# A two-layer graph kernel: the second layer's self weights folded at the start, seven early blocks, and the neighbour weights loaded behind the last store

## The chip, the cores and the metric

The kernel runs on one core of one Trainium2 chip. A core has five engines that run side by side, each in the order of its own queue: TensorE (PE: matmuls, and transposes written as matmuls), VectorE (DVE), ScalarE (ACT), GpSimd (POOL) and SyncE (SP, which here only issues transfers). Transfers (DMAs) are issued from the queues of SP, ACT and POOL. Engines and transfers wait for each other by semaphores. The metric is the device time of one execution in microseconds (us). The kernel before takes 694.12 us, the median of three runs (692.1 to 694.69).

## The reference

There are 4096 nodes with 512 features each, and an adjacency matrix of 4096 x 4096 int32 (64 MB) in which a node has about four neighbours. Layer 0 is a graph attention layer of 8 heads x 64, layer 1 averages neighbours; each is followed by a residual and a layer norm.

```python
# layer 0
Wh = einsum('nf,hfo->hno', x, W);  f1 = Wh . a[:, :64];  f2 = Wh . a[:, 64:]
e = where(adj > 0, leaky_relu(f1[:, :, None] + f2[:, None, :], 0.2), -9e15)
x = layernorm(x + heads_side_by_side(softmax(e) @ Wh))
# layer 1
agg = (adj > 0) @ x / max(degree, 1)
self_f = x @ W_self + b_self;  nb_f = agg @ W_nb + b_nb
x = layernorm(x + relu(concat(self_f, nb_f) @ W_comb + b_comb))
```

There is no nonlinearity between W_self, W_nb and W_comb. So with W_c1 and W_c2 the upper and the lower half of W_comb, layer 1 is relu(x (W_self W_c1) + agg (W_nb W_c2) + b), with b = b_comb + b_self W_c1 + b_nb W_c2. The kernel makes these two 512 x 512 products on the chip, once per execution.

## The kernel before

All work is cut into 32 blocks of 128 nodes. The queues of the engines are in the order in which the function `listed_layers` writes the operations down; nothing is reordered behind its back. Buffers come from pools that hand out the tiles of one name in turn, so an operation that writes a tile waits for the last reader of the tile that had its place. A second function with dense matmuls runs only when the lists of neighbours don't fit; it doesn't run on these inputs.

**Stage A, 0 to some 230 us: node rows and neighbour lists.** First come the heads' weights w_sb (1 MB, L817) and the first blocks of x and adj. `times` and `summed` (L838, L845) multiply W by a, so that one matmul gives a node's row: 512 features and its attention terms. The loop at L891 then runs over b = 0 to 29. In each iteration SP issues one block of x (256 KB, L314, eight blocks ahead) and adjacency block b+2 as two halves of 1 MB (`load_adj`, L384, four buffers named `at`). ACT turns each half into bf16 (`mask_adj`, L390), PE folds 128 x 4096 flags into 128 x 512 keys (`fold_adj`, L408) in a bank of PSUM that ACT fills first (`key_bank`, L400), DVE takes the largest keys (`max_keys`, L423) and decodes them to lists of neighbours (`decode`). Beside it PE transposes a block of x (`transposed`, L324) and multiplies it with W (`node_half`, L332, four matmuls of 128 x 264, twice per block), and ACT stores the row in table t0 (`store`, L885). POOL adds the blocks of x up for the row of nodes without neighbours (`sum_x`, L318). AHEAD holds the iterations that do one block of rows more. After the loop SP issues W_nb and W_c2 (`load_fold`, 2 MB, L250 and L252), the last row and the last two adjacency blocks follow, and m2 = W_nb W_c2 is made by `fold_weights`: four transposes per 128 rows (L269), a copy by ACT (L271), four matmuls of 128 x 512 (L281), a copy (L286). It is a generator: each `next` issues one piece.

**Stage B, to some 517 us: layer 0.** The loop at L967 runs over i = -2 to 32, with several blocks in different steps. POOL gathers the rows of neighbours from t0, five indirect DMAs per block (`gather`, L586), into GA = 5 buffers. A slot of 128 rows can be shared by the further neighbours of many nodes; PE adds those by a matmul with a matrix of owners (`a_shared`, L677). DVE and ACT do the softmax, weights, sums and layer norm. PE transposes the new x, SP stores it (xt, L722), and PE makes z = x m2 (`a_z`, L714), which SP stores in table t1 (L719). At i = 12 SP issues W_self and W_c1 (2 MB), and at i = 30 and 31 the bias is folded: `bias_column` (L292), `fold_bias` (four DVE operations, L300), `sum_bias` (PE, L308). While the last blocks are in work, POOL gathers for the first blocks of layer 1 (`gather_early`): from the part of t1 that is stored already (LE + b blocks for block b), with indices clamped to that limit (`lim`, `idxe`). What an early gather had to leave out is fetched by one further gather per early block (`gather_late`, NE of them).

**The seam and stage C, to the end: layer 1.** After the loop POOL issues the gathers of block 5 early and six late ones. PE makes m1 = W_self W_c1 by `fold_weights`, with `g_shared` of blocks 0 and 1 (L753) and `g_late` (L763) between its pieces, then `g_self` (x m1, L746) of blocks 0 and 1. The loop at L1082 runs over the 32 blocks: `g_self(b+2)`, `g_bias(b+3)`, `g_norm(b-1)`, `g_shared(b)`, `g_late(b)` for early blocks, `g_adds(b)`, the gathers of block b + GB into the buffer of block b (GB = 6 buffers), and `g_moments(b)` (L769, L773); `g_norm` also stores the block of the output.

Of the kernel before, what the change touches and what calls it, by code (L numbers as in the profile page):

```python
# [31 lines left out]
F32 = mybir.dt.float32  # L32
# [8 lines left out]
P = 128  # L41
# [9 lines left out]
KH = 2  # L51
# [3 lines left out]
GA = 5  # L55
GB = 6
NE = 6
LE = 26
G = 4
FMAX = 30.0  # L60
# [29 lines left out]
def listed_layers(  # L90
# [32 lines left out]
    EX = KX + 2 + 1  # L123
    AHEAD = (6, 12)
    FIRST = (0, 1, 3)
# [47 lines left out]
    for k in range(2):  # L173
# [53 lines left out]
        allow_small_or_imprecise_dtypes=True,  # L227
    )
    idxe = const.tile([P, NE, KS], U32, name="idxe")
    idxl = const.tile([P, NE], U32, name="idxl")  # L230
    esl = const.tile([P, NE, 2], F32, name="esl")
    endl = const.tile([P, NE], F32, name="endl")
    m2 = const.tile([P, FB, HD], F32, name="m2")
    brow = const.tile([P, HD], F32, name="brow")
# [12 lines left out]

    def load_fold(k, w, fp):
        wr = fp.tile([P, FB, HD], F32, name="wr")
        nc.sync.dma_start(wr, w.rearrange("(c p) o -> p c o", p=P))  # L250
        wc = fp.tile([P, FB, HD], F32, name="wc")
        nc.sync.dma_start(  # L252
            wc, w_comb[k * HD : (k + 1) * HD, :].rearrange("(c p) o -> p c o", p=P)
        )
        return wr, wc

    def load_bias(k):
        brw = small.tile([FB, P], F32, name="brw", bufs=1)
        nc.scalar.dma_start(brw, (b_self, b_nb)[k].rearrange("(c p) -> c p", p=P))
        return brw  # L260

    def fold_weights(loaded, m, wp, tags):

        wr, wc = loaded

        def turned(c):
            tp = ps.tile([P, FB, P], F32, name="sm", bufs=2)
            for d in range(FB):
                nc.tensor.transpose(tp[:, d, :], wr[:, c, ts(d, P)], ident)  # L269
            wT = wp.tile([P, FW], F32, name="row", bufs=2)[:, 0:FIN]  # L270
            nc.scalar.copy(wT, tp.rearrange("p c r -> p (c r)"))  # L271
            return wT.rearrange("p (c r) -> p c r", c=FB)

        wT = turned(0)
        for c in range(FB):
            nxt = turned(c + 1) if c + 1 < FB else None
            yield
            tag = tags[c % 2]
            mp = ps.tile([P, HD], F32, name=tag, bufs=2 if tag == "pw" else 1)
            for d in range(FB):  # L280
                nc.tensor.matmul(  # L281
                    mp, lhsT=wT[:, d, :], rhs=wc[:, d, :], start=(d == 0), stop=(d == FB - 1)
                )
                if d % 2:
                    yield
            nc.scalar.copy(m[:, c, :], mp)  # L286
            wT = nxt

    def bias_column(k, brw):

        bt = ps.tile([P, FB], F32, name="sm", bufs=2)
        nc.tensor.transpose(bt, brw, ident[0:FB, 0:FB])  # L292
        bcol = small.tile([P, FB], F32, name=f"bcol{k}", bufs=1)
        nc.scalar.copy(bcol, bt)
        return bcol
# [303 lines left out]
    def gather_early(b, pool):  # L599
        return gather(t1[0 : 2 + (LE + b) * P, :], b, pool, idxe)  # L600

# [108 lines left out]

    def a_z(b, xT, wp):
        pz = ps.tile([P, HD], F32, name="pw", bufs=2)
        for c in range(FB):
            nc.tensor.matmul(  # L714
                pz, lhsT=xT[:, c, :], rhs=m2[:, c, :], start=(c == 0), stop=(c == FB - 1)
            )
        z = wp.tile([P, HD + 2 * H], F32, name="row", bufs=2)
        nc.scalar.copy(z[:, 0:HD], pz)
        nc.sync.dma_start(t1[2 + b * P : 2 + (b + 1) * P, :], z[:, 0:HD])  # L719
# [70 lines left out]
    wp = ctx.enter_context(tc.tile_pool(name="work", bufs=1))  # L790
    fp = ctx.enter_context(tc.tile_pool(name="fold", bufs=1, side="right"))
    oo_cm = tc.tile_pool(name="owners", bufs=1, side="right")
# [17 lines left out]

    av = fp.tile([P, FB, HD], F32, name="wr")
    nc.scalar.dma_start(
# [3 lines left out]
    for h in range(H):  # L816
        nc.sync.dma_start(  # L817
            w_sb[:, :, H + h * D : H + (h + 1) * D], w0[h].rearrange("(c p) o -> p c o", p=P)
        )
    load_x(0, nc.scalar)  # L820
    load_adj(0, ap)
    load_x(1)
    load_x(2)
    load_adj(1, ap)
    for b in range(3, XL):
        load_x(b)
    xacc = xa.tile([P, FIN], F32, name="xacc")
    nc.gpsimd.memset(xacc, 0.0)
# [5 lines left out]
    xT = transposed(0, wp)  # L834
    prs = fp.tile([P, FB, HD], F32, name="wc")

# [21 lines left out]
    summed(0, 1, pr1[0])  # L858
    summed(1, 1, pr1[1])
    for b in range(XL):  # L860
        sum_x(b, xacc)
# [15 lines left out]
    def on_last(b):  # L877
        if b % G == 0:
            last[0] = fp.tile([P, G, KH * P], F32, name="wr")
        return last[0][:, b % G, :]  # L880
# [3 lines left out]
    def store(w, row):  # L884
        nc.scalar.dma_start(t0[2 + w * P : 2 + (w + 1) * P, :], row[:, 0:TW])  # L885

    for h in range(NH):
        mask_adj(0, h)
    key_bank(0)
    w, row, lists = 0, None, []  # L890
    for b in range(LB):  # L891
        for k in range(1 + (b in AHEAD)):
            load_x(w + k + XL)
            sum_x(w + k + XL, xacc)
        load_adj(b + 2, ap)
        if b == 3:
            brw = load_bias(1)
            nc.vector.memset(brow, 0.0)
            nc.scalar.dma_start(brow[0:1, :], b_comb.rearrange("(a o) -> a o", a=1))
            pads(wp)  # L900
        some(lists)
        nxt = transposed(w + 1, wp) if w + 1 < NB else None
        if w > 0:
            store(w - 1, row)
        if b + 1 < LB:
            key_bank(b + 1)
            for h in range(NH):
                mask_adj(b + 1, h)
            row = node_block(w, xT, b)
            w, xT = w + 1, nxt  # L910
        if b in AHEAD:
            nxt = transposed(w + 1, wp)
            store(w - 1, row)
            row = node_block(w, xT)
            w, xT = w + 1, nxt
        if b == 5:
            bcol = bias_column(1, brw)
        if b == 24:
            pieces = mean_row(w_sb, xacc, wp)
        if b >= 24:  # L920
            next(pieces, None)
        if b == 14:
            lates = late_lists(dp, fp.tile([P, FB * HD // P, P], F32, name="wr"))
        if b >= 14:
            next(lates, None)
        if b % G == G - 1:
            lists = [*lists[-1:], decode(b + 1 - G, dp, on_own)]
    loaded = load_fold(1, w_nb, fp)
    row = node_block(w, xT)
    store(w, row)  # L930
    fold_adj(LB - 1, dp)
    max_keys(LB - 1)
# [4 lines left out]
    G0[0] = gather(t0, 0, gps[0])  # L937
    m2s = fold_weights(loaded, m2, wp, ("pw", "pw"))
    some(lists)
    for b in (LB, LB + 1):  # L940
        key_bank(b)
        for h in range(NH):
            mask_adj(b, h)
        some(lists)
        fold_adj(b, dp)
        max_keys(b)
# [18 lines left out]
    XT, G1 = {}, {}  # L965
    biased = fold_bias(loaded, bcol)
    for i in range(-2, NB + 1):  # L967
# [27 lines left out]
        if on(i - 1):  # L995
            a_z(i - 1, XT.pop(i - 1), wp)
        if i == -2:
# [13 lines left out]
        for k in range({-2: 1, -1: 3, 0: 2}.get(i, 0)):  # L1011
            next(m2s, None)
        if 1 <= i < 12:
            some(lists)
        if 1 <= i < 5:
            next(biased)
        if i == 12:
            loaded = load_fold(0, w_self, fp)
            brw = load_bias(0)
        if i == NB - 2:  # L1020
            bcol = bias_column(0, brw)
        if i == NB - 1:
            for _ in fold_bias(loaded, bcol):
                pass
            sum_bias()
    m1 = loaded[0]


    dp_cm.__exit__(None, None, None)
    oo_cm.__exit__(None, None, None)  # L1030
    gps = [gps[(NB + b) % GA] for b in range(GA)]
    gps.append(ctx.enter_context(tc.tile_pool(name="gat5", bufs=1)))
    gl = ctx.enter_context(tc.tile_pool(name="late", bufs=1)).tile([P, NE, HD], F32, name="gl")
    G1[GA] = gather_early(GA, gps[GA])
    for b in range(NE):
        gather_late(b, gl)
    for b in range(2):
        OWN[b] = owners(b, wp)
    m1s = fold_weights(loaded, m1, wp, ("key", "tp"))
    next(m1s)  # L1040
    for b in range(2):
        g_bias(b)
        g_first(b, G1[b])
        for k in range(2):
            next(m1s)
        g_shared(b, G1[b])
        g_adds(b, G1[b], wq)
        G1[b + GB] = gather(t1, b + GB, gps[b])
        next(m1s)
    xT = load_xT(0, wp)  # L1050
    for k in range(2):
        next(m1s)
    for b in range(2):
        g_late(b, gl, wq)
    for _ in m1s:
        pass
    for b in range(2):
        nxt = load_xT(b + 1, wp)
        g_self(b, xT, m1)
        xT = nxt  # L1060
    g_bias(2)
    for b in range(2):
# [439 lines left out]
```

## Time and profile before

The profiled execution took 771.3 us, 77 us longer than the median of the timed runs. Its span on the core is 769.6 us at a mean granted TensorE clock of 0.932.

| | us | share of the span |
|---|---|---|
| median of three runs | 694.12 | |
| profiled execution, span | 771.3, 769.6 | |
| PE busy | 643.8 | 84% |
| DVE busy | 497.8 | 65% |
| ACT busy | 438.8 | 57% |
| POOL busy | 381.1 | 50% |
| stage A, 0 to 230: PE, ACT busy | 192.4, 159.5 | of 230 |
| stage B, 230 to 517: PE, POOL busy | 246.1, 175.7 | of 287 |
| seam, 517 to 567: PE, POOL busy | 43.6, 20.6 | of 50 |
| stage C, 567 to 769.6: PE, POOL busy | 161.7, 113.5 | of 202.6 |

Busy time is the time in which an engine has an instruction in execution. Idle time of an engine matters only where others wait for it, so the waits and the chain (followed back from the last instruction) are read beside the busy shares. "L586 <- PE nm L677" means that the operation of line 586 waited for the PE operation of line 677 that uses tile nm. L12 is line 12 of the kernel before. "x8" counts records; a TensorE operation on fp32 leaves two.

### The profile page before, as it was taken

How to read it: one execution, taken by the hardware profiler on the slowest of the kernel's cores; microseconds unless marked ns; L12 is line 12 of the kernel's file. 1: busy time of each engine (PE TensorE's matmuls, PEld its weight loads, DVE VectorE, ACT ScalarE, POOL GpSimd, SP SyncE). 2: the span in 40 equal slices, each digit the busy share in tenths (PEclk: the TensorE clock that was granted, in tenths of full speed). 3: DMA queues.
4: the chain of work that ended last, by engine and by line, in shares of the span. 5: the costliest groups of instructions: out<-in, count | busy, mean ns of one | idle time of the engine just before them, and what ended most of it. 6: DMA issues, size and time to landing. Idle time of an engine off the chain costs nothing.

```text
span 769.6 us, 8901 instructions
## 1 busy us (share of the span) xinstructions
PE 643.8 (84%) x2351; PEld 349.0 (45%) x2351; DVE 497.8 (65%) x1411; ACT 438.8 (57%) x923; POOL 381.1 (50%) x434
## 2 busy tenths in 40 slices
PE   3789899889968379899999999897999788978883
PEld 2557576567644144454444444443443333333331
DVE  5366888998787069988878788751335434455453
ACT  3576877768762055657666667542435444555454
POOL 6422332331117626556666665566346666766620
PEclk9899999999979679999999999998999899989897
DMA  8999999999986737778898887676467778877751
GB/s 288 387 363 406 406 407 407 407 379 379 391 332 201 205 92 238 224 235 246 280 327 248 252 265 237 218 255 210 146 187 247 240 267 275 262 248 252 253 174 59
DMA packets 93960, 209.63 MB, mean 272 GB/s; under 512 B 13633, under 2 KB 13641, under 8 KB 93902
## 3 DMA queue, kind: packets, MB, share of 16 engines
q1 hardware_dynamic: 63024, 114.05, 39.8%
q0 software_dynamic: 26080, 86.14, 37.5%
q10 hardware_dynamic: 4798, 8.80, 3.0%
q8 instruction: 21, 0.34, 0.2%
q14 instruction: 37, 0.30, 0.1%
HBM read 175.25 MB, written 33.69 MB: 272 GB/s over the span
## 4 chain that ended last, share of the span: by engine, by line
PE 37%; DVE 11%; another core or an unknown queue 9%; issue 9%; ACT 3%; DMA 2%; DVEq 0%; SPq 0%; ACTq 0%
PE pw L714 11%; PE nm L677 6%; PE pw L746 5%; PE nm L746 3%; PE tp L324 2%; PE pw L753 2%; DVE sm L769 2%; PE sm L650 2%; DVE y L733 1%; PE key L281 1%; PE sm L631 1%; PE nm L753 1%; DVE g L665 1%; DMA xT<-xt 1%
## 5 line engine op out<-in xcount | busy, mean ns | idle before, releaser
L586 POOL DMA_INDIRECT g<-t,idx x290 | 277.3, 956 | 183.9 <-issue 99.1
L390 ACT ACTIVATE ab<-at 128x2048 bf16<-128x2048 int32 x64 | 122.1, 1908 | 38.7 <-DMA at<-in_adj_dram 37.7
L332 PE MATMUL pw<-w_sb,xT 128*128 128x264 f32 x512 | 134.7, 409 | 8.9 <-DVE row L336 8.8
L714 PE MATMUL pw<-m,xT 128*128 128x512 f32 x256 | 119.4, 610 | 0.0
L332 PEld LDWEIGHTS pw<-w_sb,xT 128*128 128x128 f32 x512 | 96.7, 199 | 38.7 <-DVE row L336 10.5
L318 POOL TENSOR_TENSOR xacc<-xacc,xs 128x512 f32<-128x512 f32 x32 | 40.8, 1276 | 89.7 <-DMA xs<-in_x_dram 89.1
L665 DVE TENSOR_TENSOR g<-g,key 128x1024 f32<-128x1024 f32 x64 | 77.8, 1216 | 1.1
L746 PE MATMUL pw<-wr,xT 128*128 128x512 f32 x128 | 65.0, 656 | 13.8 <-ACT pw L737 6.8
L746 PE MATMUL nm<-wr,xT 128*128 128x512 f32 x128 | 64.2, 649 | 14.1 <-ACT nm L737 12.3
L714 PEld LDWEIGHTS pw<-m,xT 128*128 128x128 f32 x256 | 46.8, 193 | 47.5 <-issue 46.5
L324 PE MATMUL tp<-ident,xs 128*128 128x128 f32 x256 | 42.7, 292 | 30.4 <-ACT xs L709 14.8
L677 PE MATMUL nm<-g,own 128*128 128x512 f32 x128 | 64.1, 624 | 0.0
L324 PEld LDWEIGHTS tp<-ident,xs 128*128 128x128 f32 x256 | 30.6, 149 | 60.4 <-issue 29.7
L769 DVE SCALAR_TENSOR_TENSOR sm<-y,lst,nm 128x512 f32<-128x512 f32 x16 | 12.0, 753 | 67.9 <-remote 23.8
L326 ACT COPY xT<-tp 128x512 f32<-128x512 f32 x64 | 37.2, 581 | 21.3 <-PE tp L324 11.0
L746 PEld LDWEIGHTS nm<-wr,xT 128*128 128x128 f32 x128 | 26.1, 208 | 50.6 <-issue 34.4
L746 PEld LDWEIGHTS pw<-wr,xT 128*128 128x128 f32 x128 | 26.1, 210 | 50.3 <-issue 33.1
L336 DVE COPY row<-pw 128x264 f32<-128x264 f32 x64 | 26.9, 421 | 29.5 <-PE pw L332 18.9
L700 ACT ACTIVATE xs<-y,ln_sum 128x512 f32<-128x512 f32 x32 | 23.1, 723 | 37.9 <-DVE y L693 23.5
L769 DVE SCALAR_TENSOR_TENSOR sm<-y,lst,pw 128x512 f32<-128x512 f32 x16 | 12.0, 753 | 45.0 <-remote 28.0
L737 ACT COPY nm<-brow 128x512 f32<-128x512 f32 x16 | 9.4, 586 | 53.3 <-DVE sm L769 45.9
L343 POOL COPY f1s<-lst 128x24 f32<-128x24 f32 x32 | 9.7, 305 | 59.3 <-DVE fmax L340 33.4
(211 smaller groups left out, 1093.9 us busy)
## 6 DMA issues: line engine op xcount, KB each, us to landing
at<-in_adj_dram SPq DMA_DIRECT2D x64, 1024.0 KB
t<-row ACTq DMA_DIRECT2D x32, 260.0 KB
xt<-xT SPq DMA_DIRECT2D x32, 256.0 KB
t<-row SPq DMA_DIRECT2D x32, 256.0 KB
xT<-xt SPq DMA_DIRECT2D x32, 256.0 KB
out_dram<-row SPq DMA_DIRECT2D x32, 256.0 KB
xs<-in_x_dram SPq DMA_DIRECT2D x31, 256.0 KB
g<-t,idx POOLq DMA_INDIRECT x290
```

The costliest lines, as they stand in the source:

```text
L318: nc.gpsimd.tensor_tensor(xacc, xacc, xs[:, b, :], OP.add)
L324: nc.tensor.transpose(tp[:, c, :], xs[:, b, ts(c, P)], ident)
L326: nc.scalar.copy(t, tp)
L332: nc.tensor.matmul(pw, lhsT=xT[:, c, :], rhs=w_sb[:, c, k * HW : (k + 1) * HW], start=(c == 0), stop=(c == FB - 1),)
L336: nc.vector.tensor_copy(row[:, k * HW : (k + 1) * HW], pw)
L390: nc.scalar.activation(ab, loads.pop((b, h)), AF.Relu, accum_out=asum[:, b, h : h + 1])
L586: nc.gpsimd.indirect_dma_start(out=out, out_offset=None, in_=table, in_offset=bass.IndirectOffsetOnAxis(ap=at, axis=0),)
L665: nc.vector.tensor_tensor(gv if to is None else to.rearrange("p (k h d) -> p k h d", k=1, h=H), gv, E[b][:, sl].unsqueeze(3).to_broadcast( ...
L677: nc.tensor.matmul(NM[b], lhsT=OWN[b][:, k, :], rhs=G0[b][:, K0 + k, H:TW], start=False, stop=(k == KH - 1), skip_group_check=True,)
L714: nc.tensor.matmul(pz, lhsT=xT[:, c, :], rhs=m2[:, c, :], start=(c == 0), stop=(c == FB - 1))
L746: nc.tensor.matmul(NM[b], lhsT=xT[:, c, :], rhs=m1[:, c, :], start=False, stop=(c == FB - 1), skip_group_check=True,)
L769: nc.vector.scalar_tensor_tensor(yp, Y[b], lst[:, b, KL + 1 : KL + 2], NM[b], OP.mult, OP.add)
```

## The change

- **m1 at the start.** W_self and W_c1 are loaded by SP right behind w_sb, ahead of x block 1 and adjacency block 0. `fold_weights` is issued in pieces there: three behind `summed`, three behind the block of rows 0, three in each of the first iterations. It uses parts of xs, which holds x, as room for its transposes. m1 has the fixed tile that m2 had. The biases are loaded at the start, and `fold_bias` of b_self runs in iterations 0 to 3.
- **m2 over W_nb.** m2 is written over the tile that holds W_nb. `load_fold(1, w_nb)` is issued on ACT's queue behind the last `store`, not on SP's ahead of it. The rest of the bias is folded at i = 0 to 4 of stage B.
- **Early part of A.** Row block 0 and the transposes of block 1 stand before the loop, and AHEAD is one iteration (10), not two (6 and 12).
- **End of A.** `key_bank(30)` and `mask_adj(30, 0)` stand before the last store.
- **Layer 1.** GB and NE are 7, not 6; the limit of the early gathers is at most LX = 31 blocks. Layer 1 has 35 early, 7 late and 125 other gathers, where it had 30, 6 and 130. The seam has no fold any more: `g_shared`, `g_self`, `g_late` of blocks 0 and 1 follow each other.

```diff
-GB = 6
-NE = 6
+GB = 7
+NE = 7
+LX = 31
-    AHEAD = (6, 12)
+    AHEAD = 10
+    nc.vector.tensor_scalar(lim, lim, float(LX * P + 2), None, OP.min)
-    m2 = const.tile([P, FB, HD], F32, name="m2")
+    m1 = const.tile([P, FB, HD], F32, name="m1")
...
     load_x(0, nc.scalar)
+    brw = load_bias()
+    loaded = load_fold(0, w_self, fp, nc.sync)
+    load_x(1)
     load_adj(0, ap)
-    load_x(1)
     load_x(2)
+    load_x(3)
     load_adj(1, ap)
...
     summed(1, 1, pr1[1])
+    m1s = fold_weights(loaded, m1, lambda c: xs[:, NB - 12 + c, :], ("nm", "nm"))
+    for k in range(3):
+        next(m1s)
+    bcol = bias_columns(brw)
+    biased = fold_bias(loaded, bcol[:, 0:FB])
...
+    row = node_block(0, xT)
+    for k in range(3):
+        next(m1s)
+    xT = transposed(1, wp)
     for h in range(NH):
         mask_adj(0, h)
     key_bank(0)
...
+        if b < 4:
+            next(biased)
+            for k in range(3):
+                next(m1s, None)
-        if b in AHEAD:
+        if b == AHEAD:
...
-    loaded = load_fold(1, w_nb, fp)
     row = node_block(w, xT)
+    key_bank(LB)
+    mask_adj(LB, 0)
     store(w, row)
+    loaded = load_fold(1, w_nb, fp, nc.scalar)
...
+    m2 = loaded[0]
...
-        if i == 12:
-            loaded = load_fold(0, w_self, fp)
-            brw = load_bias(0)
-        if i == NB - 2:
-            bcol = bias_column(0, brw)
-        if i == NB - 1:
-            for _ in fold_bias(loaded, bcol):
-                pass
+        if i == 4:
             sum_bias()
-    m1 = loaded[0]
...
-    G1[GA] = gather_early(GA, gps[GA])
+    for b in range(GA, NE):
+        G1[b] = gather_early(b, gps[b])
     for b in range(NE):
         gather_late(b, gl)
+    xT = load_xT(0, wp)
     for b in range(2):
         OWN[b] = owners(b, wp)
-    m1s = fold_weights(loaded, m1, wp, ("key", "tp"))
-    next(m1s)
     for b in range(2):
         g_bias(b)
         g_first(b, G1[b])
-        for k in range(2):
-            next(m1s)
         g_shared(b, G1[b])
         g_adds(b, G1[b], wq)
         G1[b + GB] = gather(t1, b + GB, gps[b])
-        next(m1s)
-    xT = load_xT(0, wp)
-    for k in range(2):
-        next(m1s)
-    for b in range(2):
-        g_late(b, gl, wq)
-    for _ in m1s:
-        pass
     for b in range(2):
         nxt = load_xT(b + 1, wp)
         g_self(b, xT, m1)
         xT = nxt
+    for b in range(2):
+        g_late(b, gl, wq)
```

## The prediction

> **What bounds the kernel now.** I read the page first (busy shares, the 40 slices), then the windows of each stage, then the waits, and last the timeline and the chain around the seam between the layers, because that is where the change moves most work.
>
> The 40 slices, of 19.2 us each: PE's tenths, its granted clock, then the DMA share and rate.
>
> ```profile
> PE   3789899889968379899999999897999788978883
> PEclk9899999999979679999999999998999899989897
> DMA  8999999999986737778898887676467778877751
> GB/s 288 387 363 406 406 407 407 407 379 379 391 332 201 205 92 238 224 235 246 280 327 248 252 265 237 218 255 210 146 187 247 240 267 275 262 248 252 253 174 59
> ```
>
> Stage A is bound by the adjacency stream: 406 to 407 GB/s, and nowhere more. After slice 12 the rate falls to some 240 GB/s, so stages B and C are not bound by it. Slice 29 (146 GB/s) is the seam. The windows, with busy time and count of PE, PEld, DVE, ACT and POOL, then clock, DMA share, GB/s:
>
> ```profile
> 60.00:110.00 50.00, 44.93 (x260) 33.32 (x259) 39.17 (x138) 37.85 (x47) 15.61 (x22) 1.00 1.05 407
> 340.00:360.00 20.00, 18.14 (x68) 9.52 (x68) 17.67 (x41) 12.92 (x34) 11.40 (x12) 1.00 0.74 224
> 547.00:567.00 20.00, 20.00 (x48) 8.93 (x47) 5.03 (x12) 8.63 (x21) 0.81 (x2) 1.00 0.40 120
> 640.00:660.00 20.00, 16.53 (x35) 6.95 (x35) 9.83 (x21) 9.55 (x26) 13.38 (x15) 0.91 0.77 254
> ```
>
> In A PE is busy 45 of 50 us, so there is little slack for additional PE work. In B PE sets the pace. In 547 to 567 PE is full and POOL is empty. The waits say what POOL waits for (total, times, longest):
>
> ```profile
> POOL g L586 <- PE nm L677: 43.6, 16, 13.3
> ...
> POOL g L586 <- PE nm L753: 19.2, 1, 19.2
> ```
>
> In B, POOL waits for PE (L677 frees gather buffers). In C, it waits once, 19.2 us. In the timeline of POOL, bracketed idle time stands last:
>
> ```profile
> 530.30 0.95 POOL L586 DMA_INDIRECT gl<-t,idxl  x1 [0.30 <-issue]
> 535.33 0.95 POOL L586 DMA_INDIRECT g<-t,idx  x1 [4.08 <-ACT wr L286]
> ...
> 566.79 0.95 POOL L586 DMA_INDIRECT g<-t,idx  x1 [19.19 <-PE nm L753]
> 568.04 0.94 POOL L586 DMA_INDIRECT g<-t,idx  x1 [0.31 <-issue]
> ```
>
> One gather takes 0.95 + 0.30 = 1.25 us of POOL, so five take 6.27 us per block. PE's part of a later block is L746 3.43 + L753 1.72 = 5.15 us, so undisturbed C runs at POOL's rate. The chain (start, us, what) shows what PE does meanwhile; POOL idles 23.3 us in all:
>
> ```profile
> 523.24 6.15 PE key L281 x8
> ...
> 543.73 3.43 PE tp L281 x8
> 547.17 3.43 PE nm L746 x8
> 550.60 3.43 PE pw L746 x8
> ```
>
> The fold of W_self W_c1 stands before all g_self, and block 2's shared product (564.17 to 566.05) stands behind both.
>
> The profiled execution took 771.3 us (span 769.6), 77 more than the median of 694.12. The chain puts 8.7%, 67 us, on "another core or an unknown queue": pauses such as 10.5 us at 599 and 8.8 at 623, whose releaser the trace doesn't name. Their sum is close to the 77 us, so I estimate that the timed runs mostly lack them, and cost C from rates rather than from its profiled length.
>
> **What the Trainium skill says.** "DMA: Bandwidth & Descriptors", section "Issuing engines are not separate DMA queues": DMAs of scalar, sync and gpsimd run on the same 16 DMA engines and interleave. So moving W_nb's 2 MB from SP's queue to ACT's adds no bandwidth; the 407 GB/s ceiling with SP, ACT and POOL all issuing agrees. "Perfetto Trace Analysis", section "DMA Instruction — SWDGE (GPSIMD)": the record of such a DMA ends when its descriptors are written, not when the data lands. The trace agrees: records take 0.95 us, landings come some 3 us after issue. "TensorE: Matmul & The Clock Gate", Part 1: an idle PE drops to half clock, and warms after about 3.4 us of work. The trace agrees at 523.24: eight L281 records took 6.15 us after 5.24 idle, 3.43 to 3.45 us afterwards.
>
> **The change, part by part.**
>
> *Start of A.* It adds 2 MB (W_self, W_c1) ahead of x1 and adj 0. At 407 GB/s that is +5.2 us. The traffic isn't new, it leaves B, but only A is bound by it. It also adds the fold to PE: 16 transposes (L269, 1.04 us per 8: 2.1) and 16 fp32 matmuls (L281, four in 3.43: 13.7). Half of it stands, in order, before the first mask: on PE eight transposes, one L281 group, node block 0 (3.04 + 2.05 us at L332), four transposes, another group; ACT's copies of these stand before mask(0,0). W_c1 lands at about 12.2 (before, adj 0's first half let its mask start at 13.13; w_sb's 1 MB ahead is unchanged). From 13.7: 1.5 + 3.43 to 6.15 + 5.1 + 0.5 + 3.43 + the copies gives mask(0,0) at 27 to 31 us against 13.13. SP's first wait for an adjacency buffer comes after some 9 MB, at about 25 us. So the stream runs dry for 2 to 6 us: I take 4. The other half of the fold stands in iterations 0 and 1, where PE has slack while ACT catches up. Against it, dips of the old start (24 to 30 us, 42 to 51 us: together 2.8 us of lost rate) fall into this one; I count 2 of them gone. A starts +7 us late, bounds +3 and +15.
>
> *AHEAD.* One extra node block instead of two in the loop, one in front: same work. Nothing, as each transfer is the same; the price if not is one late mask (2 us), within the bounds.
>
> *End of A.* Mask(30,0) and its key copy (1.9 + 0.6 us) move into ACT's wait before store(31); ACT idles 7.2 us there (221.41, for DVE lst L339), which hides them. Store(31) stays on ACT, so what follows it comes earlier by 2.5 us, less about 1 us for issuing two DMAs. W_nb lands later, some 226 to 228, and the m2 fold, the next that needs it, starts after mask 31. −1.4; bounds −3 to +4 if the fold waits.
>
> *B.* Four L300 (0.75 us), L308 and L292 leave its end: −1.1. 2 MB leave at i=12, which had cost a late gather: −0.5. m2 in another tile and the bias pieces at i=0 to 3: nothing, as DVE has 2.3 of 20 us free there, and the same four ran at 1 to 4.
>
> *Seam and C.* T is the end of B (last L714, 517.1). Before, undisturbed, PE does fold 2.1 + 0.5 copy wait + 13.7, L753 3.4, L763 1.7, five L746 17.2, L753 1.7 = 40.4, with 1.2 of waits: T + 41.6. Then POOL: 120 × 1.253 = 150.4, to T + 192.3, +3 landing, +11.8 for the last shared product, moments, norm and store = T + 207. After: PE does L753 3.4, two L746 6.9, then waits. POOL issues G(5) to T + 6.7, G(6) to T + 13.0, seven late to T + 21.8; the second late one lands at T + 17.4. Then L763 1.7, three L746 10.3, L753 1.7: T + 31. Meanwhile blocks 7 and 8 need buffers of blocks 0 and 1, free since T + 4. They end at T + 34.3, after T + 31, so POOL does not wait at all: 125 × 1.253 = 156.6, to T + 178.4, and the end T + 193.2. That is −13.8. PE's own sum in C comes to T + 193 as well, so POOL and PE are now equal, and each jitter of one shows: I give back 1.5. C: −12.3; bounds −19 (profiled, L753 of block 2 ends at T + 49, hence 18 later than T + 31) and −6 (PE's limit alone before, T + 199).
>
> *Sum.* +7 − 1.4 − 1.6 − 12.3 = −8.3. On the profiled time 771.3 it is about 763, or 757 if C's pauses hang on the seam as they did. On the median: 694.1 − 8.3 = 686.
>
> **Rivals.**
>
> *C gains all that the profile shows (−18 to −19).* For it: gather end to moments lags 33 to 37 us all through C, so consumption, not POOL, sets the profiled pace; a consumer that starts 18 us earlier ends 18 us earlier. Against: the pauses make that lag. It gives 694.1 + 7 − 3 − 18.5 = 680.
>
> *The start eats the gain.* PE folds at half clock (6.15 us a group), mask(0,0) at 31 to 33, the stream is dry for 8: S = 5.2 + 8 = 13 to 15, less 3, less 12.3: 692 to 694. For: PE waits with gaps over 3 us there. Against: node block 0 keeps it busy between the groups.
>
> *Slower.* In A, PE has 5 of 50 us free and ACT 12, so a start that is late is only caught up at that slack. If mask(0,0) comes at 38 or later, because the first four groups' order holds ACT behind PE (m1's copies, biases, brow), the stream loses 13 us or more, S = 19 to 25, and C's −12 does not pay: 698 to 704. It decides from S = 15.3, a first mask at about 34.
>
> *It doesn't do what it says.* The table t1 may not be ready for G(6) early: no, its limit is the same 31 blocks as G(5)'s. But a wait of G(7) on a buffer, or PE waiting for late gathers (T + 12 to T + 17.4) with a cold restart, would keep C at −6: 692.
>
> **How the numbers follow.** Chances: my forecast (681 to 690) 0.50; the larger gain (674 to 681) 0.14; start or C eats it (690 to 697.6) 0.20; slower 0.16. I say 686; own range 681 to 690. Eight in ten: leaving out about a tenth on each side, 676 to 700. Half a per cent, 3.5 us, is about what a measurement of this kernel can tell from no change: faster (below 690.6) 0.66, same 0.17, slower (over 697.6) 0.17.
>
> **What would show it.** In the changed profile: mask(0,0) at 27 to 31 us and a slice 1 to 2 with a low rate; SP's last adjacency half landing 5 to 9 us later than 222.7; the first gather of layer 0 some 4 us later than 228.1; no L281 after the last L714 of B; block 2's L753 about 31 us after it; no POOL idle over 1 us between G(5) and the tenth block; the span 8 to 15 us shorter. Wrong would be: a POOL wait <- PE L753 in C of more than 5 us, a stream dry after 40 us, or a first mask after 34.

## The result, and the profile after

The changed kernel takes 695.10 us (median of 20 runs), the kernel before 695.14 beside it: ratio 0.9996, 95% interval 0.9975 to 1.0017. Nothing is gained. The forecast was 686.

The profile of before that the prediction was read from has 67 us of pauses in its chain, which the timed runs lack. A second profile of the kernel before has a span of 690.1 us without them; all comparisons below use that second profile. (One whole series of runs, told of below, had such pauses too, in every kernel.)

The 40 slices of the page, 17.3 us each: first the kernel before, second profile, then the changed kernel (span 693.8 us). The rows are PE's busy tenths, the DMA share, and GB/s.

```profile
PE   3797989797996989899999999999999999999992
DMA  8999999999999678886899999978856899999983
GB/s 287 387 359 407 407 407 407 406 407 388 385 404 364 194 220 266 267 251 214 258 311 355 281 282 274 281 238 286 258 165 189 286 311 309 310 309 309 299 296 120
```

```profile
PE   5997989879899688999999999999869999999992
DMA  8899999999999977888788999978988899999991
GB/s 269 327 382 320 399 406 407 407 407 385 322 404 375 347 232 230 273 262 255 214 260 277 273 280 281 272 253 263 307 241 266 282 306 317 311 305 304 305 305 72
```

At the seam (slices 30 and 31) the rate no longer falls to 165 and 189: the gain is there. But the adjacency stream is poorer at the start (slices 2 to 4 carry 327, 382 and 320 GB/s, before 387, 359 and 407) and in slice 11 (322, before 385), and it ends a slice later: slice 14 still carries 347 GB/s, where before it carried 194. With T the end of stage B (the last x m2), the trace gives this account:

| | before | changed | difference | forecast |
|---|---|---|---|---|
| first mask starts | 12.7 | 30.5 | +17.8 | at 27 to 31 |
| last mask ends | 229.0 | 242.7 | +13.7 | |
| T | 481.5 | 492.9 | +11.4 | +4 |
| from T to the end | 208.7 | 200.9 | −7.8 | −12.3 |
| span | 690.1 | 693.8 | +3.7 | −8.3 |

Both halves missed to the same side. Of the 17.8 us by which the first mask is later, 6.9 are not the fold's: in `fold_away` (below), with neither the loads nor the fold, it starts at 19.6: row block 0 and the transposes of block 1 now stand before it in the queues. The forecast priced that move at nothing, and T doesn't show a price for it either (479.5 there).

Single profiles scatter: four kernels with the same stages A and B had T at 489.9 to 494.4. So medians of timed runs carry the sums, and profiles the places. The runs of different experiments come from different chips, on which the kernel before had medians of 693.99 to 695.14 (one chip, told of below, apart). A difference of medians from two experiments is uncertain by that much, so the difference of their ratios to the kernel before, measured beside each, is given too.

POOL's waits at the seam have gone, as forecast. Before (second profile), then changed, in the view of waits (total, times, longest):

```profile
POOL g L586 <- PE nm L753: 17.1, 2, 16.8
```

```profile
POOL g L591 <- PE nm L682: 22.5, 21, 3.8
...
PE nm L768 <- DMA gl<-t,idxl: 5.5, 1, 5.5
```

A rival that the forecast named has taken their place: PE waits 5.5 us for a late gather. The timeline of PE shows where (start, us, operation, idle time before it), changed kernel:

```profile
503.01 3.60 PE L751 MATMUL pw<-m,xT 128*128 128x512 f32 x8
512.13 2.04 PE L768 MATMUL nm<-gl,ol 128*128 128x512 f32 x2 [5.52 <-DMA gl<-t,idxl]
513.97 1.92 PE L768 MATMUL pw<-gl,ol 128*128 128x512 f32 x2
515.67 3.67 PE L751 MATMUL nm<-m,xT 128*128 128x512 f32 x8
...
527.70 1.88 PE L758 MATMUL nm<-g,own 128*128 128x512 f32 x4
```

The two products behind the wait take 2.04 and 1.92 us, where 1.02 is usual: PE has become slow in the gap (the granted clock is 0.52 from 512 to 516 us). The last line is block 2's shared product, which has to be done before POOL can gather another block into block 2's buffer; it ends at T + 36.7.

### The profile page after: what moved, and what is told of

Same layout as the page of the kernel before. It is cut to its first block, busy times and chain, and to the rows that moved or that the text cites. A ratio compares the mean times of both kernels' runs of the same rounds, so it can differ in the third digit from the quotient of the medians.

```text
span 693.8 us, 8911 instructions
## 1 busy us (share of the span) xinstructions
PE 620.6 (89%) x2354; PEld 340.8 (49%) x2354; DVE 495.9 (71%) x1415; ACT 439.1 (63%) x922; POOL 383.4 (55%) x435
## 4 chain that ended last, share of the span: by engine, by line
PE 50%; DVE 22%; DMA 9%; issue 6%; POOL 4%; ACT 4%; DVEq 0%; ACTq 0%; SPq 0%; POOLq 0%
PE pw L719 11%; PE pw L337 7%; PE nm L751 6%; PE nm L682 6%; PE pw L751 6%; POOL g L591 4%; PE pw L758 3%; PE nm L758 3%; DMA xT<-xt 2%; PE tp L329 2%; DMA g<-t,idx 2%; DVE row L341 2%; DMA t<-row 2%; PE sm L655 1%; DVE kk L428 1%
## 5 line engine op out<-in xcount | busy, mean ns | idle before, releaser
L591 POOL DMA_INDIRECT g<-t,idx x285 | 272.4, 956 | 109.6 <-issue 71.0
L337 PE MATMUL pw<-w_sb,xT 128*128 128x264 f32 x512 | 131.9, 403 | 15.8 <-DVE row L341 15.8
L719 PE MATMUL pw<-wr,xT 128*128 128x512 f32 x256 | 117.7, 602 | 0.7 <-ACT xT L331 0.7
L719 PEld LDWEIGHTS pw<-wr,xT 128*128 128x128 f32 x256 | 46.3, 190 | 47.3 <-issue 46.1
L751 PE MATMUL nm<-m,xT 128*128 128x512 f32 x128 | 58.0, 596 | 4.5 <-DMA xT<-xt 4.5
L751 PE MATMUL pw<-m,xT 128*128 128x512 f32 x128 | 57.8, 594 | 1.5 <-ACT nm L742 1.5
L329 PE MATMUL tp<-ident,xs 128*128 128x128 f32 x256 | 40.2, 280 | 7.1 <-ACT xs L714 5.8
L751 PEld LDWEIGHTS nm<-m,xT 128*128 128x128 f32 x128 | 24.1, 191 | 37.3 <-issue 32.1
L591 POOL DMA_INDIRECT g<-t,idxe x35 | 33.1, 947 | 15.4 <-issue 8.5
L751 PEld LDWEIGHTS pw<-m,xT 128*128 128x128 f32 x128 | 24.1, 190 | 32.2 <-issue 28.4
## 6 DMA issues: line engine op xcount, KB each, us to landing
xs<-in_x_dram SPq DMA_DIRECT2D x31, 256.0 KB, 12.7
```

Of the source, the lines that this page charges most:

```text
L329: nc.tensor.transpose(tp[:, c, :], xs[:, b, ts(c, P)], ident)
L337: nc.tensor.matmul(pw, lhsT=xT[:, c, :], rhs=w_sb[:, c, k * HW : (k + 1) * HW], start=(c == 0), stop=(c == FB - 1),)
L591: nc.gpsimd.indirect_dma_start(out=out, out_offset=None, in_=table, in_offset=bass.IndirectOffsetOnAxis(ap=at, axis=0),)
L719: nc.tensor.matmul(pz, lhsT=xT[:, c, :], rhs=m2[:, c, :], start=(c == 0), stop=(c == FB - 1))
L751: nc.tensor.matmul(NM[b], lhsT=xT[:, c, :], rhs=m1[:, c, :], start=False, stop=(c == FB - 1), skip_group_check=True,)
```

## The experiments

**The price of the start, and its halves.** `fold_away` has neither the 2 MB of W_self and W_c1 at the start nor the fold; `load_only` has the loads alone. Both leave out the product W_self W_c1 (m1 is W_self), so their times are those of the rest. `fold_away` also lacks the four bias pieces of b_self and loads W_self in stage B.

```diff
 # fold_away
-    loaded = load_fold(0, w_self, fp, nc.sync)
-    m1s = fold_weights(loaded, m1, ...)     # and every next(m1s), next(biased)
+        if i == 12:
+            nc.sync.dma_start(m1, w_self.rearrange("(c p) o -> p c o", p=P))
 # load_only
-    loaded = load_fold(0, w_self, fp, nc.sync)
+    nc.sync.dma_start(m1, w_self.rearrange("(c p) o -> p c o", p=P))
+    wc1 = fp.tile([P, FB, HD], F32, name="wc")
+    nc.sync.dma_start(wc1, w_comb[0:HD, :].rearrange("(c p) o -> p c o", p=P))
+    loaded = (None, wc1)
-    m1s = fold_weights(loaded, m1, ...)     # and every next(m1s)
```

> The kernel before, unchanged, for a profile without the pauses that made the first one 77 us longer than the timed runs. If the pauses belong to that one execution: span 690 to 696; layer 0 (stage B) ends at 480 to 486 us and the rest takes 205 to 210 (the estimate of the prediction: T + 207). If they belong to the kernel: span over 750 again.

> The changed kernel without the 2 MB of W_self and W_c1 at the start and without their fold (m1 is W_self itself, loaded in stage B; the product W_self W_c1 and its bias part are left out). Theory 1 (the seam gains about 10 us and the start costs as much): 683 to 686 us. Theory 2 (the seam and stage C gain almost nothing, because PE sets their end anyhow, and the start costs almost nothing): 692 to 695.

> The changed kernel with the 2 MB loaded at the start as there, but without the fold on PE and ACT (W_self goes to the tile of m1; the product is left out). If the price of the start is the bandwidth: as the changed kernel, 693 to 696. If it is PE's and ACT's order of work: near the kernel without both, and above it by the 5.2 us that 2 MB take at 407 GB/s at most: 686 to 690.

Measured: the kernel before 690.1 us of span, T at 481.5 and 208.7 from there (the forecast's model had T + 207). `fold_away` 680.36 us, 0.9797 (0.9752 to 0.9841); `load_only` 682.29, 0.9825 (0.9782 to 0.9869). So the start costs 695.10 − 680.36 = 14.7 us: 1.9 for the 2 MB, 12.8 for the fold. By the ratios it is 13.8 us, 1.9 and 11.9 (0.9797, 0.9825, 0.9996). T says much the same: 479.5, 482.2, 492.9, so 2.7 and 10.7. Theory 1 holds for the price of the start, and is even short. The bandwidth that the forecast charged with 5.2 is not the main price.

Where the price of the fold arises is seen in the windows of stage A (length, then busy time of PE, PEld, DVE, ACT, POOL, clock, DMA share, GB/s), `load_only` and then the changed kernel:

```profile
30.00:34.00 4.00, 4.00 (x29) 2.93 (x29) 2.64 (x8) 0.76 (x2) 3.84 (x3) 1.00 1.07 410
34.00:54.00 20.00, 15.22 (x76) 10.29 (x75) 8.69 (x26) 13.74 (x16) 8.74 (x11) 0.83 1.05 406
54.00:74.00 20.00, 16.13 (x90) 11.14 (x89) 16.85 (x65) 16.18 (x21) 4.40 (x6) 1.00 1.05 406
74.00:110.00 36.00, 33.09 (x196) 24.94 (x195) 27.40 (x109) 27.04 (x33) 10.88 (x16) 1.00 1.05 407
```

```profile
30.00:34.00 4.00, 2.98 (x18) 1.95 (x19) 0.43 (x1) 4.00 (x4) 3.84 (x5) 1.00 0.47 120
34.00:54.00 20.00, 19.57 (x96) 12.30 (x96) 6.19 (x22) 15.22 (x21) 5.96 (x6) 1.00 1.01 372
54.00:74.00 20.00, 16.09 (x89) 11.04 (x88) 12.87 (x52) 14.91 (x20) 5.69 (x6) 0.91 0.93 324
74.00:110.00 36.00, 32.65 (x190) 24.41 (x189) 26.75 (x109) 26.81 (x36) 10.41 (x17) 1.00 1.05 407
```

Against 407 GB/s the changed kernel loses 4 × (410 − 120)/407 = 2.9 us up to 34, 20 × 34/407 = 1.7 up to 54, and 20 × 82/407 = 4.0 up to 74: 8.6 us. From 74 to 144 us both run at 407, about the most that any window shows, so nothing of it comes back there: a stream at its ceiling can't make up time in which it ran dry. By the bytes moved up to 215 us the changed kernel is 10.1 us behind `load_only`, close to the 10.7 by which its T is later (another 3 us are lost from 144 to 200, and 1.8 come back up to 215, where `load_only` runs at 357 GB/s). The 2.9 + 1.7 are the dry start that the forecast charged with 2 to 6; the 4.0 after 54 us are not in it. Iterations 0 and 1, with the second half of the fold, take 7.7 us each (masks of blocks 1, 2, 3 at 34.7, 42.4 and 50.2 us), longer than the 6.4 us for a block that `load_only` takes where its stream sets the pace (masks of blocks 8 and 9 at 73.6 and 80.0). That the 4.0 come from this alone isn't shown: a wait of SP falls into the same stretch (told under the padding rows).

**Seven blocks or six.**

```diff
 # six
-GB = 7
-NE = 7
+GB = 6
+NE = 6
```

> The changed kernel with six early blocks and six buffers in layer 1, all else as there. If POOL's gathers set the end of stage C, POOL waits for block 2's shared product again (some 9 us) and the time rises by 4 to 6. If PE sets it: within 2 us of the changed kernel.

Measured: 688.97 us, 0.992 (0.990 to 0.994), 6.1 below the changed kernel (5.3 by the ratios). No expectation had a gain. In its trace, PE does the late products of blocks 0 and 1 at T + 13.5 without a wait and at full clock, and block 2's shared product ends at T + 30.0, not 36.7:

```profile
504.44 3.60 PE L751 MATMUL pw<-m,xT 128*128 128x512 f32 x8
507.87 1.02 PE L768 MATMUL nm<-gl,ol 128*128 128x512 f32 x2
508.73 1.02 PE L768 MATMUL pw<-gl,ol 128*128 128x512 f32 x2
```

From T to the end it takes 196.6 us, where the changed kernel takes 200.9. The seventh block has put five gathers (6.3 us of POOL) ahead of all late gathers. From this came the next experiment.

**The late gathers first.**

```diff
 # late_first
+    for b in range(NE):
+        gather_late(b, gl)
     for b in range(GA, NE):
         G1[b] = gather_early(b, gps[b])
-    for b in range(NE):
-        gather_late(b, gl)
```

> The changed kernel with the seven late gathers ahead of the gathers of blocks 5 and 6 on POOL's queue; all else as there. Theory 1 (the seam lost its gain because PE waits for the late gathers of blocks 0 and 1, which stand behind ten gathers of 1.25 us): PE's wait of 5.5 us goes, 688 to 690 us. Rival (the seventh buffer itself costs, by memory traffic or by its place): within 2 us of the changed kernel, 693 to 696.

> The changed kernel with the same pieces of the fold in groups of three, but all behind the first mask, in iterations 0 to 4. If the fold costs 10.7 us because it holds back the first mask (30.5 us) and the stream runs dry: most of it comes back, 685 to 688. If it costs because PE's 15.8 us of work have no room in stage A wherever they stand: 693 to 696.

> The changed kernel with one piece of the fold in each of iterations 0 to 12 (at most 1.72 us of PE and one copy each) and none ahead of the first mask. If the lateness of the first mask and of the fifth iteration costs: 683 to 687. If PE's work as such costs: 691 to 696.

> The same spread fold with six early blocks and six buffers. If the two prices add: spread minus 6 us (what six blocks gave alone), 678 to 682 where spread gives 684 to 688. If they share one cause: no more than 2 us below the better of the two.

These four ran on a chip where every kernel paused as in the first profile: the kernel before took 780.94 us there (71 runs), `late_first` 780.47 (ratio 1.0012, 0.998 to 1.0045), `behind_mask` 785.59 (1.013), `spread` 783.81 (1.0123) and `spread_six` 783.54 (1.0029). The two variants of the fold came out 1.2 to 1.3% slower there, clear of noise, and faster on the other chips (below); why is not known. The argument rests on the second series:

> The changed kernel with the seven late gathers ahead of the gathers of blocks 5 and 6, again, since every kernel of the first try, the kernel before among them, took some 780 us with long pauses. Theory 1 (PE waits at the seam for late gathers that stand behind ten others): PE's wait of 5.5 us goes, 688 to 690 us, 0.991 to 0.994 of the kernel before. Rival (the seventh buffer itself costs): 0.997 to 1.002.

Measured: 693.95 us, 0.9994 (0.9965 to 1.0024). Theory 1 failed as stated, and the rival seemed right. The trace says otherwise. PE's wait has gone (block 2's shared product ends at T + 29.5), but POOL now stands still. The timeline of POOL, `late_first_b`:

```profile
494.26 0.95 POOL L591 DMA_INDIRECT g<-t,idxe  x1 [0.30 <-DMA t<-row]
500.60 0.95 POOL L591 DMA_INDIRECT gl<-t,idxl  x1 [5.38 <-DMA t<-row]
```

A late gather reads all of t1, so it waits for t1's last store. The gathers of block 5 had covered that wait. Now POOL's last gather ends at T + 184.1, not T + 181.8, and the end comes at T + 199.9. So stage C has two bounds close to each other: PE's wait in the changed kernel (T + 200.9), POOL's here. Six blocks had neither wait.

**Block 5, then the late ones, then block 6.**

```diff
 # late_mid
-    for b in range(GA, NE):
-        G1[b] = gather_early(b, gps[b])
+    G1[GA] = gather_early(GA, gps[GA])
     for b in range(NE):
         gather_late(b, gl)
+    for b in range(GA + 1, NE):
+        G1[b] = gather_early(b, gps[b])
```

> The changed kernel with POOL's order at the seam: gathers of block 5, the seven late gathers, gathers of block 6. Theory 3 (stage C has two bounds that lie 4 us apart: PE, late by its wait for late gathers behind ten others, in the changed kernel; POOL, idle 5.4 us for the last store of t1, when the late ones come first): both go, from T (the end of stage B) to the end 193 to 197 us instead of 200.9, 688 to 691 us, 0.991 to 0.995 of the kernel before. Rival (seven buffers or gathers cost in themselves): 199 us or more from T, 0.998 to 1.001.

Measured: 688.43 us, 0.9917 (0.9895 to 0.9938); 195.1 us from T to the end. Theory 3 holds. At the seam POOL doesn't wait once (0.30 us between all gathers), and block 2's shared product on PE ends at T + 31.1. POOL's timeline, then PE's line of that product:

```profile
495.95 0.94 POOL L591 DMA_INDIRECT g<-t,idxe  x1 [0.30 <-issue]
497.19 0.95 POOL L591 DMA_INDIRECT gl<-t,idxl  x1 [0.30 <-issue]
...
504.69 0.95 POOL L591 DMA_INDIRECT gl<-t,idxl  x1 [0.30 <-issue]
505.95 0.95 POOL L591 DMA_INDIRECT g<-t,idxe  x1 [0.30 <-issue]
```

```profile
519.10 1.88 PE L758 MATMUL nm<-g,own 128*128 128x512 f32 x4
```

POOL's last gather ends at T + 178.5. The same gathers in another order, with nothing taken away, are worth 6.7 us (5.5 by the ratios). The seventh block is then worth nothing that can be measured: six blocks gave 688.97.

**Where the fold stands.** All variants keep the loads at the start.

```diff
 # behind_mask: the six pieces ahead of the first mask go to iterations 0 to 4, three each
-    for k in range(3):
-        next(m1s)        # behind summed, and again behind node_block(0)
+        if b < 5:
+            for k in range(3):
+                next(m1s, None)
 # spread: one piece in each of iterations 0 to 12
+        if b < 13:
+            next(m1s, None)
 # spread_six: spread with GB = NE = 6; spread_mid, behind_mid: with late_mid's order
```

> The fold in groups of three pieces in iterations 0 to 4, none ahead of the first mask, again. If the fold costs 10.7 us by holding back the first mask: 0.986 to 0.991 of the kernel before. If PE's 15.8 us of work have no room in stage A wherever they stand: 0.998 to 1.002.

> One piece of the fold in each of iterations 0 to 12, again. If lateness at the start costs: 0.983 to 0.989 of the kernel before. If PE's work as such costs: 0.995 to 1.002.

> The spread fold with six early blocks, again. If the two prices add: 6 us below the spread fold alone, 0.976 to 0.982 of the kernel before. If they share one cause: within 2 us of the better of the spread fold (above) and six blocks (0.992).

> The same order with the fold spread over iterations 0 to 12. If the two prices are apart and add: 5 to 6 us below late_mid, 681 to 685 us, level with the spread fold and six blocks (684.05) or 1 to 3 below. Rival: no better than the spread fold alone (690).

> The same order with the fold in groups in iterations 0 to 4. As the spread one, 681 to 685 us, if PE's lateness at the start is made up by then either way; above it by 2 to 4 if the groups hold back the first masks again.

| | us | of before | 95% | beside it, fold at the start: by medians; by ratios |
|---|---|---|---|---|
| behind_mask_b | 688.68 | 0.9935 | 0.9911 to 0.9960 | changed kernel 695.10: −6.4; −4.2 |
| spread_b | 690.00 | 0.9938 | 0.9916 to 0.9959 | changed kernel: −5.1; −4.0 |
| spread_six_b | 684.05 | 0.9870 | 0.9814 to 0.9927 | six 688.97: −4.9; −3.5 |
| spread_mid | 684.27 | 0.9863 | 0.9817 to 0.9909 | late_mid 688.43: −4.2; −3.7 |
| behind_mid | 685.21 | 0.9863 | 0.9806 to 0.9919 | late_mid: −3.2; −3.7 |

So the place of the fold is worth 3 to 6 us, less than the 10.7 (by T) that would make place its whole price, but clearly not nothing: the expectations at both ends missed (0.9935 and 0.9938 lie between them). Groups or single pieces make no difference that can be told. The two prices add: `spread_six_b` is 5.9 below `spread_b` (4.7 by the ratios; its own ratio, 0.987, missed the expected 0.976 to 0.982, which took a larger gain of the spread fold for granted). The rest of the fold, some 6 to 10 us, was paid wherever the fold stood in stage A; that PE's work as such is the price, and not ACT's copies, was not tried apart. `spread_b` loses hardly more stream time than `load_only` up to 144 us (0.5 us by the bytes moved), and more of it later; its windows and those of `load_only`:

```profile
144.00:170.00 26.00, 21.34 (x118) 15.67 (x116) 22.35 (x79) 15.66 (x20) 5.20 (x8) 0.87 0.89 324
170.00:200.00 30.00, 27.06 (x167) 20.10 (x165) 27.09 (x106) 24.84 (x31) 7.53 (x15) 1.00 1.01 356
```

```profile
144.00:170.00 26.00, 22.00 (x139) 16.49 (x139) 23.85 (x91) 17.92 (x23) 9.12 (x12) 1.00 1.05 406
170.00:200.00 30.00, 28.89 (x175) 20.79 (x175) 25.65 (x113) 25.60 (x31) 4.80 (x10) 1.00 1.03 386
```

Lateness of the masks is hidden while there are loaded buffers ahead, and seems to come out in a later stretch, where DVE is busy 22 of 26 us with lists and copies (24 of 26 in `load_only`). That this is how it is paid is read from the trace and not tried.

**The padding rows.** The chain of the changed kernel runs through 11.6 us of transfers in iteration 4, where the padding of the tables takes a row tile:

```profile
54.55 6.35 DMA t<-row
...
62.17 5.29 DMA t<-row
67.46 0.03 issue
```

```diff
 # pads_away
-        pad = wp.tile([P, FW], F32, name="row", bufs=2)
+        pad = xs[:, NB - 14 : NB - 12, :].rearrange("p b f -> p (b f)")
```

> The changed kernel with the padding rows of the tables (iteration 4) made in an unused part of xs, not in a row tile, so that neither the padding waits for the last store nor the next row for the padding's stores (6.35 and 5.29 us in the chain from 54.5 to 67.5 us). If this wait, no longer covered once the first mask is late, is part of the start's 10.7 us: 690 to 692 us, 0.993 to 0.997 of the kernel before, and the end of stage B 2 to 5 us earlier than 492.9. If PE's late work would have filled that time anyhow: 694 to 696.

> The same padding with the fold spread over iterations 0 to 12 and POOL's order of late_mid. There the stream lost nothing before 130 us, so if the padding's wait was covered: 683 to 685 us, as without it; if it set the lateness that is paid after 144 us: 679 to 682.

> The same padding with the fold in groups in iterations 0 to 4 and POOL's order of late_mid. There the stream lost 2.6 us between 50 and 66 us: if by the padding's wait, 681 to 683 us; else 684 to 686.

Measured: `pads_away` 694.65 us, 0.9991 (0.9970 to 1.0011); `spread_mid_pads` 686.45 (0.9866), above both expected ranges, `behind_mid_pads` 686.41 (0.9882). Not the cause: here a place on the chain was no price. With the padding away the rate in 54 to 74 us is 332 GB/s, hardly more than 324. In both kernels SP's queue stands still there for one load of x that waits for a row store to land (6.4 us in the changed kernel), with the next adjacency loads behind it. The changed kernel, then `load_only`, in the view of waits:

```profile
SPq L319 <- DMA t<-row: 6.4, 1, 6.4
SPq L319 <- DMA t<-row: 4.4, 1, 4.4
```

So `load_only` has such a wait too (from 47.0 to 51.4 us), and its stream keeps 406 GB/s; and `behind_mask_b`, with the groups in iterations 0 to 4, has 0.9 us of it and still falls to 332 GB/s from 54 to 74 us. The wait alone is no cause, and a loss of that size arises without it. What it adds in the changed kernel was not tried.

## Why the prediction was wrong

**Right.** The model of the kernel before from T on (T + 207, measured 208.7); that the pauses are no part of the timed runs; that the first mask comes at 27 to 31 us (30.5) and a fold group runs at half clock (6.45 us); that the stream then runs dry for 2 to 6 us (4.6 up to 54 us); that POOL's long idle time at the seam goes; that the ends of A and B give a little (`fold_away` has T 2.0 before that of the kernel before; forecast 3).

**Wrong, first step: "The other half of the fold stands in iterations 0 and 1, where PE has slack while ACT catches up."** It has none there. PE is busy 19.6 of the 20 us from 34 to 54, the two iterations take 7.7 us against the stream's 6.4, and 4.0 us more of stream are lost from 54 to 74 us (SP's wait may have a part in them). In `behind_mask_b`, where the groups stand in iterations 0 to 4, PE is busy all of the 40 us from 34 to 74. The deeper error is the notion of catching up. The forecast counted PE's 5 free us in 50 as room, but the stream runs at its ceiling, so once it has run dry only the work behind it can catch up, not the stream. The fold costs 12 to 13 us where I had charged some 4 for it; the load costs 1.9 where I had charged 5.2. The start is 13.4 to 14.7, not 7; its bound of 15 held it. One sign of being wrong that the forecast named came: a stream dry after 40 us.

**Wrong, second step: "the second late one lands at T + 17.4. Then L763 1.7, three L746 10.3, L753 1.7: T + 31."** The order was read, and PE's idle time in it was priced too low. The late products started at T + 19.2: the first late gather landed 5.4 us after it was issued (the seven have a median of 4.5), where the forecast reckoned with some 3. They took 3.5 us at a low clock, not 1.7. The three products of L746 (here L751) took 12.0, not 10.3, 1.4 of it a wait for a load of xT. So block 2's shared product ended at T + 36.7, not T + 31. I had set the sums of PE and POOL level (both T + 193) and given back 1.5 us for it. In the order of `late_mid` that product ends 5.6 us earlier, at T + 31.1, and the end comes 5.8 earlier: by these two profiles the wait on PE is paid in full. There POOL's last gather ends at T + 178.5, forecast T + 178.4, and the end comes at T + 195.1, forecast 193.2: the sum was about right for an order in which nobody waits for late gathers, and the change doesn't have that order. This is the rival "PE waiting for late gathers (T + 12 to T + 17.4) with a cold restart, would keep C at −6"; it came at −7.8.

**The sum again.** By the profiles: start +13.4 (T of the changed kernel less T of `fold_away`), ends of A and B −2.0, stage C −7.8: +3.6, which is the difference of the two spans (+3.7) taken apart and no test of it. The medians of 20 runs differ by nothing. The profiled execution of the kernel before took 691.86 us, 3.3 below that median, the one of the changed kernel 695.46, 0.4 above its own: the distance lies in which executions were profiled. By the timed runs the kernel without the start, `fold_away`, is 14.1 us below the kernel before (95%: 11.0 to 17.2), where the forecast had 15.3 for the ends and stage C together, and the start takes 13.8 back. So the start is the step whose miss is sure and large. How much stage C gave by itself is not settled more closely; that its order left 5.5 to 6.7 us behind is measured by `late_mid`. Of the cases on record, "start or C eats it (690 to 697.6)", at 0.20, was the one that came, and it was both.

**Still open.** Why spreading the fold and putting it behind the first mask give 3.2 to 6.4 us and no more is read from the trace alone; the load of x that waits for a store wasn't taken away; and why 2 MB more at the start cost 1.9 us and not 5.2 wasn't looked into.

## What to carry to other kernels

Work moved off one critical stretch has to be priced where it lands, and a stage whose transfers already run at their ceiling is the dearest place: PE's idle share there is no room, because a stream at its ceiling can't run faster later. Put such work behind the first consumers of the stream: here that gave back 3 to 6 us of 12 to 13, in groups as well as in single pieces. When gathers are added to an in-order queue, ask who waits for what stands behind them: the same gathers in another order were worth 5.5 to 6.7 us, and the seventh buffer they served was worth nothing. The best version measured has six blocks and the fold spread (684.05 us, 0.987 of the kernel before, four runs); with seven and the better order it is level (684.27, four runs).

## What the runs showed of the hardware

On one chip every kernel took 780 to 786 us where on others it takes 684 to 695: pauses, the longest ones in `late_first` 5 to 18 us, in which the trace names no engine of the core as releaser. A profile from such a chip can be read for the order of events, not for lengths, and two variants that are 0.6% faster elsewhere were 1.2 to 1.3% slower there.

The granted clock matters in short gaps. After 5.5 us of idle time, two products of 0.86 us each became 1.7 to 1.8 us, so a wait on PE cost its length and some 2 us more. The length of a gap does not decide it alone: the eight records of a product of L751 took 5.40 us in `late_mid` after 1.97 us of idle time, but 3.70 in `fold_away` after 1.99, and 3.60 is usual. In these traces the clock is halved for stretches of 3.41 us or multiples of it. At the seam that came after a stretch of 3.41 us in which PE was busy 1.44 us (`late_mid`), 1.10 (`fold_away`) or 1.03 (changed kernel), and not after one with 1.69 (`fold_away`). So PE need not be idle throughout to be slowed. Where the limit lies wasn't tried.
